# A Mamba block followed by linear attention on one core: the folds of the scanned states put first, TensorE's side work kept to its budget, and ScalarE's passes limited to two in a slot

## The chip, the core and the metric

The kernel runs on one NeuronCore of a Trainium2 chip. TensorE (PE, with its weight loads as PEld), VectorE (DVE), ScalarE (ACT) and GpSimd (POOL) each work off their own queue of instructions in order; SyncE (SP) issues most transfers. The metric is the device time of one execution, in microseconds (us), as the median of several runs. The kernel before takes 7723.51 us (median of three runs, 7722.88 to 7725.43).

## What is computed

The input is x, 4 batches of 512 channels by 4096 positions, in float32. Two layers, each added to its own input, with a norm over groups of 16 channels ahead of each:

```python
# layer 0, for each group of 128 channels ("chunk")
xn = layer_norm(group_norm(x))            # over 512 channels
xi, z = split(xn_chunk @ in_proj)         # 256 + 256 channels
xc = silu(causal_conv4(xi) + conv_b)
dt, B, C = split(xc @ x_proj);  dt = softplus(dt @ dt_proj + dt_b)
h[l] = exp(dt[l] * A) * h[l-1] + (dt[l] * xc[l]) * B[l]     # 256 channels x 16 states
y[l] = sum over states of h[l] * C[l]  +  xc[l] * D
x = x + proj(layer_norm(out_proj(y * silu(z)) + skip * xn_chunk))
# layer 1
q, k, v = group_norm(x) @ w_qkv;  q, k = relu(q), relu(k)
x = x + w_out @ ((v @ (k^T q)) / norm)    # linear attention, 8 heads
```

The recurrence over l is the heart: 4 batches x 4 chunks x 256 channels x 16 states, each a chain over 4096 positions.

## The kernel before

**Slots.** Positions are cut into tiles of 512. A *step* is one (batch, tile, chunk): 128 steps in all. A step has 16 *slots*: two halves `e` of the 256 channels, four groups `q` of four states, two halves `jj`. In each slot (`slot`, L837) VectorE makes two scans of 128 rows x 512 positions (L846), each from a decay `dA` that ScalarE makes in PSUM (`decay`, L820, three ahead, three banks) and an input `bx` that GpSimd makes (`drive`, L828, two slots ahead, three buffers).

**Pairs.** Two slots make a *pair*, with one buffer `h` of four scanned rows of 512; there are two such buffers. The states of a pair are then multiplied by C: positions 0 to 383 by VectorE (`product`, L866) with `c_all`, which TensorE spreads into the one bank of `ps_c` (`c_row`), and positions 384 to 511 by GpSimd (L858). Then TensorE adds them up over the states into the bank `y` with four small matmuls (`fold_states`, `y<-h,fold`). The product and the fold of a pair are issued in the first slot of the next pair, after its first scan, but after its second scan in slot 10. So the scan that opens pair k must wait until the fold of pair k-2, which reads the same `h`, is done; that fold is queued one pair earlier, behind its product. In `fold_states` the order on TensorE is: `c_row` for the next pair; where a half `e` begins (the folds issued in slots 2 and 10) also `diagonal`, four small matmuls that start bank `y` with xc * D; then the four folds. `take_y` (ScalarE, slots 0 and 8) reads the one bank `y` out.

**The work around the scans.** All else is written out by hand in `after` (L1323), which runs at the end of each slot: the projections of the step after next (slots 3 to 9), time steps with two table loads around a softplus (slot 3), out-projection (slot 4), a silu with two table loads (slot 10), and so on. Three queues of generators give further pieces: `ahead` (norms of the next tile), `late` (norm and projection of the finished tile) and `rest` (the attention of the batch before). In every slot each queue may give one piece, if its last `yield` allows it: kind "free" goes always, "wide" only at set slots, and other pieces of `late` and `rest` only while `credit` is positive. `credit` gains 3.5 matmuls a slot less what was spent, at most 2.6. A piece of kind "more" (the second half of a group of four matmuls) also goes without credit, if no other queue has issued more than one matmul in the slot. In the slots after 3 and 10 a "free" piece may go twice. `clear` (L108) keeps ScalarE's norm and statistics passes out of slots 3 and 10 (`AWAY`). The passes are L397 (group norm, in two groups of two), L474 and L515 (squares), L485 (layer norm's scale) and L661 (sums and squares for the next norm). `fetch` (L929) lets a tile for the attention land for two slots before it is used.

After the last slot the attention of the last batch runs alone, nearly all of it on TensorE.

Of the kernel before, what the change touches and what calls it, by code (L numbers as in the profile page):

```python
# [8 lines left out]
F32 = mybir.dt.float32  # L9
# [5 lines left out]
P = 128  # L15
T = 512
# [8 lines left out]
def kernel(  # L25
# [48 lines left out]

    held, now, due = [0], [None], []

    def work_bank(name, behind=1):
        held[0] += behind  # L80
# [26 lines left out]

    def clear():  # L108

        while now[0] is not None and now[0] % SLOTS in AWAY:  # L110
            yield "wait"

    def pause(n):
        return until(later(n, lambda: None))
# [272 lines left out]
    def group_norm(dst, xt, norm):  # L387
        gr, off, _ = norm
        for c in range(NC):
            if c % 2 == 0:  # L390
                yield from clear()
            if now[0] is None and c % 2:
                nc.vector.tensor_scalar(
                    dst[:, c, :], xt[:, c, :], gr[:, c : c + 1], off[:, c : c + 1], ALU.mult, ALU.add
                )
            else:
                nc.scalar.activation(  # L397
                    dst[:, c, :], xt[:, c, :], AF.Identity,
                    bias=off[:, c : c + 1], scale=gr[:, c : c + 1],
                )  # L400
            if c == 1:
                yield "free"
        yield
# [53 lines left out]
    def layer_norm(v, name):  # L457
        while norming:
            yield "wait"
        norming.append(name)  # L460
        yield from room()
        sums = work_bank(f"mu_sums_{name}")
        sums_into(sums, [v[:, c, :] for c in range(NC)], range(NC))
        mu = yield from mean_of(sums, f"mu_{name}", "one ahead")
        yield "wide"
        over(v, mu, ALU.subtract)
        free()
        yield "free"
        sqs = []
        for c in range(NC):  # L470
            if c % 2 == 0:
                yield from clear()
            sqs.append(wk.tile([P, T], F32, tag="sq", name=f"sq_{name}_{c}", bufs=4))
            nc.scalar.activation(sqs[c], v[:, c, :], AF.Square)  # L474
            if c == 1:
                yield "free"
        yield from room()
        sums = work_bank(f"var_sums_{name}")
        sums_into(sums, sqs, range(NC))
        var = yield from mean_of(sums, f"var_{name}", "two ahead")  # L480
        yield from over_deviation(v, var, name)
        for c in range(NC):
            if c % 2 == 0:
                yield from clear()
            nc.scalar.activation(  # L485
                v[:, c, :], v[:, c, :], AF.Identity,
                bias=b_sb[:, c : c + 1], scale=g_sb[:, c : c + 1],
            )
            if c % 2:
                yield "free"  # L490

    def layer_scale(v, name):
# [19 lines left out]

        def part(c):
            sqs[c] = wk.tile([P, T], F32, tag="sq", name=f"sq_{name}_{c}", bufs=4)
            nc.scalar.activation(sqs[c], v[:, c, :], AF.Square, bias=about)  # L515

        yield from clear()
# [127 lines left out]
    def shifted(f, xt, t, nm):  # L645
# [11 lines left out]
        for o in range(NC):  # L657
            yield from clear()
            for v, func in (("sum", AF.Identity), ("square", AF.Square)):
                unused = wk.tile([P, T], F32, tag="res", name=f"{v}_{nm}_{o}", bufs=2)  # L660
                nc.scalar.activation(  # L661
                    unused, xt[:, o, :], func, bias=f["off"][:, o : o + 1],
                    accum_out=f[v][:, o, t : t + 1],
                )
            yield "free"
# [202 lines left out]
    def fold_states(g, last):  # L868

        n, e, q, _ = place(g)  # L870
        if g + 1 < last:
            c_row(g + 1)
        if q == 0:
            ys[n, e] = ps_y.tile([P, T], F32, tag="y", name=f"y_{n}_{e}")
            diagonal(ys[n, e], dg[:, e, :], fs[n]["xz"][:, 0, e, :])
        h = hs.pop(g // JJ)
        for j in range(NJ):
            mm(
                ys[n, e][j * BLK : (j + 1) * BLK, :], fold, h[:, j, :],
                start=False, stop=(q == NQ - 1), abreast=NJ,  # L880
            )


    def take_y(f, n, e):
        nc.scalar.copy(f["xz"][:, 0, e, :], ys.pop((n, e)))  # L885
# [31 lines left out]
    def attention(b, x1s, stats):  # L917
# [12 lines left out]
        def fetch(t, why, spare=1):  # L930

            if t < NT and t not in tiles and not no_tile(spare):
                x1 = load_now(x1s[t], f"x{why}_{b}_{t}")
                tiles[t] = x1, pause(2)

        def fetched(t, why):
            fetch(t, why)
# [365 lines left out]
    with tc.manual_schedule():  # L1303
        credit, seen, mix, held[0], held_x[0] = 0.0, work["mm"], iter(()), 0, 0
        for n, (b, t, c) in enumerate(steps):
# [10 lines left out]
            for s in range(SLOTS):  # L1316
                def after():
                    nonlocal credit, seen
                    now[0] = n * SLOTS + s
                    for what in [w for at, w in due if at <= now[0]]:  # L1320
                        what()
                    due[:] = [d for d in due if d[0] > now[0]]
# [130 lines left out]
```

## Time and profile before

| | |
|---|---|
| median of 3 runs | 7723.51 us |
| the profiled execution | 7720.72 us, of it a span of 7718.9 us |
| mean granted TensorE clock | 0.914 |
| busy: PE / DVE / ACT / POOL | 83% / 90% / 71% / 89% of the span |
| scans run from / to | 91.6 us / 7293.4 us |
| the four batches, from first scan to the next batch's first | 1757.6, 1815.9, 1815.9, 1810.0 us |
| after the last scan | 425.5 us |

A page gives busy times over the whole span; here some 92 us at the start and 425 us at the end belong to other work, so VectorE and GpSimd are fuller in the loop than the page's shares. In the lists of waits, a row gives the waiting engine and line, who ended the wait, the total, the number and the longest. In the timelines the columns are start, length, engine, line, operation, tiles, shapes and count, and in brackets the idle time of the engine just before and who ended it. A matmul of 128x512 float32 stands there as two records.

### The profile page before, as it was taken

How to read it: one execution, taken by the hardware profiler on the slowest of the kernel's cores; microseconds unless marked ns; L12 is line 12 of the kernel's file. 1: busy time of each engine (PE TensorE's matmuls, PEld its weight loads, DVE VectorE, ACT ScalarE, POOL GpSimd, SP SyncE). 2: the span in 40 equal slices, each digit the busy share in tenths (PEclk: the TensorE clock that was granted, in tenths of full speed). 3: DMA queues.
4: the chain of work that ended last, by engine and by line, in shares of the span. 5: the costliest groups of instructions: out<-in, count | busy, mean ns of one | idle time of the engine just before them, and what ended most of it. 6: DMA issues, size and time to landing. Idle time of an engine off the chain costs nothing.

```text
span 7718.9 us, 91874 instructions
## 1 busy us (share of the span) xinstructions
PE 6424.2 (83%) x25496; PEld 2090.3 (27%) x25528; DVE 6951.6 (90%) x5720; ACT 5466.3 (71%) x8384; POOL 6892.8 (89%) x4638
## 2 busy tenths in 40 slices
PE   5677777677789988988788988898788889898799
PEld 1111212111223322322222333332122323232244
DVE  6999999999999999999999999999999999999821
ACT  5677777777777777777777777777777777777521
POOL 5999999999999999999999999999999999999700
PEclk8788888888899999999899999999899999999799
DMA  6666666666666666676666666677666665677502
GB/s 176 168 171 168 158 151 160 163 159 169 174 171 169 164 170 167 181 196 168 175 167 174 178 165 163 164 187 194 161 172 165 161 161 150 168 191 192 141 33 93
DMA packets 829222, 1265.43 MB, mean 164 GB/s; under 512 B 184072, under 2 KB 317720, under 8 KB 816416
## 3 DMA queue, kind: packets, MB, share of 16 engines
q1 hardware_dynamic: 806352, 1225.99, 60.8%
q0 software_dynamic: 16368, 32.51, 2.4%
q8 instruction: 200, 3.28, 0.2%
q14 instruction: 318, 2.61, 0.1%
q10 hardware_dynamic: 5984, 1.06, 0.1%
HBM read 1052.25 MB, written 206.57 MB: 163 GB/s over the span
## 4 chain that ended last, share of the span: by engine, by line
DVE 35%; PE 29%; ACT 11%; DMA 8%; issue 7%; POOL 7%; SPq 2%; DVEq 0%; POOLq 0%; ACTq 0%
DVE h L846 22%; DVE h L866 10%; PE pc L129 6%; PE y L129 5%; PE pq L129 5%; POOL bx L828 5%; ACT dA L820 4%; DMA d_all<-d_rows 3%; PE pr L129 3%; PE po L129 3%; PE pp L129 2%; SPq L795 2%; DVE xn L439 2%; DMA c_sb<-c_rows 2%; DMA b_all<-b_rows 1%
## 5 line engine op out<-in xcount | busy, mean ns | idle before, releaser
L828 POOL TENSOR_TENSOR bx<-d_all,b_all 128x1024 f32<-128x1024 f32 x2048 | 4824.6, 2368 | 147.2 <-DVE h L846 130.3
L846 DVE TENSOR_TENSOR_SCAN h<-dA,st,bx 128x512 f32<-128x512 f32 x3584 | 4352.3, 1267 | 309.7 <-ACT dA L820 101.9
L820 ACT ACTIVATE dA<-d_all,a_t 128x512 f32<-128x512 f32 x4096 | 2756.9, 688 | 1408.1 <-DVE h L846 1351.8
L866 DVE TENSOR_TENSOR h<-h,c_all 128x1536 f32<-128x1536 f32 x1024 | 1770.5, 1729 | 0.1
L858 POOL TENSOR_TENSOR h<-h,c_sb 128x512 f32<-128x512 f32 x1024 | 1299.8, 1269 | 99.7 <-DMA c_sb<-c_rows 15.9
L129 PE MATMUL y<-h,fold 128*32 128x512 f32 x8192 | 1249.3, 685 | 43.9 <-POOL h L858 42.3
L129 PE MATMUL c_all<-parts,sel 128*128 128x384 bf16 x1024 | 366.1, 358 | 939.2 <-DVE h L866 936.8
L129 PE MATMUL pc<-xn,w_cv 128*128 128x512 f32 x2048 | 1037.4, 640 | 129.1 <-DVE xn L439 79.7
L129 PE MATMUL pq<-w_qk,xa 128*128 128x512 f32 x2048 | 953.3, 601 | 5.1 <-ACT xa L397 2.5
L846 DVE TENSOR_TENSOR_SCAN h<-dA,bx 128x512 f32<-128x512 f32 x512 | 590.7, 1205 | 39.0 <-PE y L129 15.7
L129 PEld LDWEIGHTS pc<-xn,w_cv 128*128 128x128 f32 x2048 | 385.0, 199 | 735.3 <-issue 408.1
L129 PEld LDWEIGHTS <-sel 128*128 128x128 bf16 x1216 | 120.4, 99 | 1606.3 <-DVE h L866 1392.2
L129 PEld LDWEIGHTS pq<-w_qk,xa 128*128 128x128 f32 x2048 | 389.8, 193 | 453.7 <-issue 435.6
L129 PE MATMUL pr<-xb,m 128*128 128x512 f32 x1024 | 475.8, 603 | 3.4 <-ACT res L1136 2.6
L129 PE MATMUL pp<-xn,w_pr 128*128 128x512 f32 x1024 | 477.4, 596 | 0.0
L129 PE MATMUL y<-xz,dg 32*32 32x512 f32 x2048 | 346.2, 752 | 0.0
L888 POOL TENSOR_TENSOR xz<-xz 128x512 f32<-128x512 f32 x256 | 325.4, 1271 | 11.2 <-ACT xz L885 11.2
L129 PEld LDWEIGHTS y<-h,fold 128*32 128x32 f32 x8192 | 169.6, 113 | 611.5 <-issue 381.4
L731 POOL TENSOR_TENSOR dt<-dt,xz 128x1024 f32<-128x1024 f32 x127 | 299.9, 2361 | 0.8 <-ACT dt L723 0.6
L129 PE MATMUL pd<-xz,w_xp 128*128 128x512 f32 x512 | 294.7, 704 | 0.0
L129 PE MATMUL pz<-xn,w_z 128*128 128x512 f32 x512 | 271.5, 623 | 6.5 <-ACT kq L959 4.8
L129 PEld LDWEIGHTS pr<-xb,m 128*128 128x128 f32 x1024 | 192.8, 193 | 253.9 <-issue 226.9
(226 smaller groups left out, 5965.4 us busy)
## 6 DMA issues: line engine op xcount, KB each, us to landing
d_all<-d_rows SPq DMA_DIRECT2D x2040, 256.0 KB, 4.3
b_all<-b_rows SPq DMA_DIRECT2D x4096, 64.0 KB, 2.4
d_rows<-dt SPq DMA_DIRECT2D x254, 512.0 KB, 2.8
c_sb<-c_rows SPq DMA_DIRECT2D x4096, 16.0 KB, 3.5
xn<-in_x_dram SPq DMA_DIRECT2D x32, 1024.0 KB, 7.1
x<-xr SPq DMA_DIRECT2D x32, 1024.0 KB, 4.2
xa<-x SPq DMA_DIRECT2D x32, 1024.0 KB, 5.2
xb<-x SPq DMA_DIRECT2D x32, 1024.0 KB, 5.8
```

The lines of the kernel that those rows point to most:

```text
L129: nc.tensor.matmul(out_, lhsT, rhs, **how)
L439: nc.vector.tensor_tensor(v, v, bc(m, NC), op)
L731: nc.gpsimd.tensor_tensor(f["both"][:, 1], f["both"][:, 0], f["xz"][:, 0], ALU.mult)
L795: nc.sync.dma_start(dst[k * BLK : (k + 1) * BLK, :], rows_[q * KS + k, :].partition_broadcast(BLK))
L820: nc.scalar.activation(dAs[k], fs[n]["d_all", e][:, 0, j, :], AF.Exp, scale=a_t[:, e, j, q : q + 1])
L828: nc.gpsimd.tensor_tensor(bxs[g], fs[n]["d_all", e][:, 1, jj * 2 : jj * 2 + 2, :], bc(b_all[g // JJ], 2), ALU.mult)
L846: nc.vector.tensor_tensor_scan(h[:, j, :], dAs.pop(2 * g + i), bxs[g][:, i, :], 0.0 if t == 0 else st[:, c, e, q, j : j + 1], ALU.mult, AL ...
L858: nc.gpsimd.tensor_tensor(h[:, :, CUT:], h[:, :, CUT:], bc(c_sb.pop(g // JJ), NJ), ALU.mult)
L866: nc.vector.tensor_tensor(own, own, bc(c_all.pop(g // JJ), NJ), ALU.mult)
L888: nc.gpsimd.tensor_tensor(f["xz"][:, 1, e, :], f["xz"][:, 1, e, :], f["xz"][:, 0, e, :], ALU.mult)
```

## The change

There are five edits.

1. `fold_states`: the four folds come first, `c_row` for the next pair after them. `diagonal` leaves this function and becomes `begin_y`, called at the end of slots 1 and 9, after all other pieces of the slot.
2. In slots 3 to 8 (`heavy`) a new piece of `late` or `rest` needs a credit above 1 instead of above 0, and a "more" piece needs a credit above 0.
3. `fetch` lets a tile land for three slots instead of two.
4. A counter `passes`, cleared in each slot and raised by each of ScalarE's norm and statistics passes of whatever queue.
5. `clear` also holds a generator back, with kind "free", while `passes` is above 1; it is asked before each group of passes.

```diff
     def clear():
-        while now[0] is not None and now[0] % SLOTS in AWAY:
-            yield "wait"
+        while now[0] is not None and (now[0] % SLOTS in AWAY or passes[0] > 1):
+            yield "wait" if now[0] % SLOTS in AWAY else "free"
...
+                passes[0] += 1
                 nc.scalar.activation(
                     dst[:, c, :], xt[:, c, :], AF.Identity,
...
         n, e, q, _ = place(g)
-        if g + 1 < last:
-            c_row(g + 1)
-        if q == 0:
-            ys[n, e] = ps_y.tile([P, T], F32, tag="y", name=f"y_{n}_{e}")
-            diagonal(ys[n, e], dg[:, e, :], fs[n]["xz"][:, 0, e, :])
         h = hs.pop(g // JJ)
         for j in range(NJ):
             mm(
                 ys[n, e][j * BLK : (j + 1) * BLK, :], fold, h[:, j, :],
                 start=False, stop=(q == NQ - 1), abreast=NJ,
             )
+        if g + 1 < last:
+            c_row(g + 1)
+
+    def begin_y(n, e):
+        ys[n, e] = ps_y.tile([P, T], F32, tag="y", name=f"y_{n}_{e}")
+        diagonal(ys[n, e], dg[:, e, :], fs[n]["xz"][:, 0, e, :])
...
-                tiles[t] = x1, pause(2)
+                tiles[t] = x1, pause(3)
...
                     now[0] = n * SLOTS + s
+                    passes[0] = 0
...
-                    busy = False
+                    busy, heavy = False, int(3 <= s < 9)
...
-                        if queue is ahead or kind == "free" or credit > 0 or kind == "more" and not busy:
+                        if queue is ahead or kind == "free" or credit > (kind != "more") * heavy or kind == "more" and not (busy or heavy):
...
+                    if s % (SLOTS // NH) == 1:
+                        begin_y(n, s // (SLOTS // NH))
                     seen = work["mm"]
```

The line `passes[0] += 1` also stands before each of the passes at L474, L485, L515 and L661 (the last with two passes a group).

More of the change, by code (lines that the diff above doesn't have):

```diff
@@ L73 @@
     ps_w = ctx.enter_context(tc.tile_pool(name="ps_w", bufs=3, space=bass.MemoryType.PSUM))
-    held, now, due = [0], [None], []
+    held, now, due, passes = [0], [None], [], [0]
     def work_bank(name, behind=1):
@@ L473, in layer_norm @@
             sqs.append(wk.tile([P, T], F32, tag="sq", name=f"sq_{name}_{c}", bufs=4))
+            passes[0] += 1
             nc.scalar.activation(sqs[c], v[:, c, :], AF.Square)
@@ L484, in layer_norm @@
                 yield from clear()
+            passes[0] += 1
             nc.scalar.activation(
@@ L514, in part @@
             sqs[c] = wk.tile([P, T], F32, tag="sq", name=f"sq_{name}_{c}", bufs=4)
+            passes[0] += 1
             nc.scalar.activation(sqs[c], v[:, c, :], AF.Square, bias=about)
@@ L659, in shifted @@
             for v, func in (("sum", AF.Identity), ("square", AF.Square)):
+                passes[0] += 1
                 unused = wk.tile([P, T], F32, tag="res", name=f"{v}_{nm}_{o}", bufs=2)
```

## The prediction

> **What bounds the kernel now.** First the page's busy line and its groups, to see which engines are full.
>
> ```profile
> PE 6424.2 (83%) x25496; PEld 2090.3 (27%) x25528; DVE 6951.6 (90%) x5720; ACT 5466.3 (71%) x8384; POOL 6892.8 (89%) x4638
> L828 POOL TENSOR_TENSOR bx<-d_all,b_all 128x1024 f32<-128x1024 f32 x2048 | 4824.6, 2368 | 147.2 <-DVE h L846 130.3
> L846 DVE TENSOR_TENSOR_SCAN h<-dA,st,bx 128x512 f32<-128x512 f32 x3584 | 4352.3, 1267 | 309.7 <-ACT dA L820 101.9
> ```
>
> VectorE and GpSimd are nearly equally full, and the loop of 2048 slots takes 7202 us (91.6 to 7293.4). Of VectorE's idle time some 349 us stand before the scans (309.7 here, 39.0 in the group without `st`). That is all there is to win on VectorE, so the second view is its list of waits:
>
> ```profile
> DVE h L846 <- PE y L129: 114.1, 112, 4.5
> DVE h L846 <- ACT dA L820: 104.6, 110, 3.5
> DVE h L846 <- POOL st L857: 38.7, 43, 2.2
> DVE h L846 <- ACT xn L899: 28.4, 30, 2.7
> DVE h L846 <- POOL bx L828: 26.4, 34, 2.2
> DVE h L846 <- ACT kq L954: 22.5, 8, 3.0
> ```
>
> A scan waits on several semaphores, and the named line is only the last event near its start: no scan needs L899, L954 or slot 11's L857. So I paired the trace's 4096 scans in order of issue with their dA, bx and the fold of the pair two back, and took for each idle stretch what ended last. From the third pair on, VectorE's idle time before scans is 346 us: **fold late 234.5, dA late 87.8, bx late 22.3**. By the slot of the waiting scan the folds cost 80.4 (slot 12), 87.9 (slot 8), 22.8 (slot 10), 18.2 (6), 14.7 (4) and 10.6 (the rest); dA costs 29.5 (5), 10.6 (6), 7.3 (7), 8.1 (10), 7.1 (12), 23.2 (13), 2 elsewhere.
>
> Third, the timeline shows why. Slots 4 to 8 of a step with attention:
>
> ```profile
> 2204.09 1.98 PE L129 MATMUL po<-xz,w_op 128*128 128x512 f32 x4
> 2204.53 1.73 DVE L866 TENSOR_TENSOR h<-h,c_all 128x1536 f32<-128x1536 f32 x1
> ...
> 2205.91 1.88 PE L129 MATMUL pp<-xn,w_pr 128*128 128x512 f32 x4
> ...
> 2211.06 0.33 PE L129 MATMUL c_all<-parts,sel 128*128 128x384 bf16 x1
> ...
> 2211.32 1.06 PE L129 MATMUL y<-h,fold 128*32 128x512 f32 x8
> ...
> 2212.55 1.28 DVE L846 TENSOR_TENSOR_SCAN h<-dA,st,bx 128x512 f32<-128x512 f32 x1 [2.74 <-ACT xn L899]
> ```
>
> The product ends at 2206.26, but TensorE is still at out-projection and side work and begins the fold 5.06 us later; the scan starts 0.17 us after the fold's end. Without stall the scan comes 3.46 us after the product (three scans; 2.37 us for slot 10's fold, which has two). Slot 10's fold:
>
> ```profile
> 3017.71 0.34 PE L129 MATMUL c_all<-parts,sel 128*128 128x384 bf16 x1
> 3017.97 1.06 PE L129 MATMUL y<-xz,dg 32*32 32x512 f32 x8
> 3018.97 1.06 PE L129 MATMUL y<-h,fold 128*32 128x512 f32 x8
> ```
>
> Even begun at once, it ends 2.4 us after its product, against 2.37 us of room. And dA: six passes in one slot hold ScalarE's queue (first column start, second length):
>
> ```profile
> 2966.97 0.71 ACT L661 ACTIVATE sum<-xr,moff 128x512 f32<-128x512 f32 x1
> 2968.38 2.92 ACT L397 ACTIVATE xa<-xa,off_b,gr_b 128x512 f32<-128x512 f32 x4
> 2971.91 1.28 DVE L846 TENSOR_TENSOR_SCAN h<-dA,st,bx 128x512 f32<-128x512 f32 x1 [3.47 <-ACT dA L820]
> ```
>
> **The change part by part.** No arithmetic is added or removed; the instructions of each kind are as many, but for about 1010 more semaphore waits each on PE and VectorE (the fold now waits for VectorE itself, the product for `c_row`). VectorE's recurring order keeps its slots, so this is about TensorE's and ScalarE's places.
>
> *Folds first, diagonals a slot earlier.* The fold of slot 10 starts 0.26 + 1.00 us sooner after its product, and so does slot 2's. Subtracting 1.4 us (the two rows' lengths) from each of the 78 stalls of slot 12 leaves 10.4 of 80.4 us, and behind them 6.3 of dA show up: 16. Slot 4: 14.7 to 0. Elsewhere a fold gains 0.34 us. `c_row` is now 1.06 us later, but its product comes a scan after the next fold's deadline: nothing. The diagonal goes to the end of slots 1 and 9, where TensorE had on average 1.0 and 2.4 us of work; it waits for `take_y` of the slot before, behind which only that slot's `c_row` and fold are queued: nothing, or if ScalarE is late the wait it had before.
>
> *No overdraft.* Counting each slot's matmuls at the rows' lengths (0.94 us for 128x512 float32, 1.06 for four small ones) in the two orders, for batches 1 and 2: slots 2 to 4 fall from 12.8 to 10.9 us (the slots take 11.8), slots 5 to 9 go from 15.4 to 16.8 (17.4). Runs of three slots with over 12 us of matmuls fall from 202 to 124. Slot 6's fold, behind slots 2 to 5, comes 0.34 us sooner by its order and up to 1.9 by the load: stall at slot 8 87.9 becomes 20 (subtracting 1.4 from each of its 66 stalls; 11 with 1.9, 66 with 0.34). Slot 8's fold has 0.7 us more before it in slots 6 and 7 and less backlog: 22.8 becomes 17. Slots 6, 14, 0: 7 of 29. Folds in all: 234.5 to 60, a gain of 175; with the order's 0.34 us alone for slots 6, 8, 10 and 14 it is 120.
>
> *Two passes a slot.* Slots with four or more passes fall from 103 to none (one has three). The excess of six passes over two is 4 x 0.7 to 0.8 = 3 us, as large as the stalls of 1.3 to 3.5 us at slot 13: 23 becomes 5; slot 6's, up to 2.8 us behind four passes, go from 10.6 to 3. Slot 5's dA waits for slot 3's table loads, begun late because a `pq` queued behind slot 2's diagonal was late: 1.06 us sooner takes 29.5 to about 5, of 27 stalls up to 2 us. The other 24.5 stay: dA 88 to 37, gain 51. Held passes shift the next tile's norm by one slot, and attention ends at slot 1011 instead of 992 (batch 0's), with 76 slots to spare; batch 2's at 2024 of 2048. The tail has the same 130 ScalarE instructions: 0.
>
> *Longer landing.* The chain of waits has three `xb` landings of 8.1 to 9.8 us, over two slots (7.1): 0 to 5 us. I take 0, since TensorE's waits name no DMA.
>
> *More semaphore waits.* Those before the scans take 21 ns each: 1010 on VectorE cost 0 to 21 us. I take 0, as they pass while the previous scan runs (back-to-back starts overlap by 83 ns with and without one).
>
> **Where the stall goes.** Gross the sum is 175 + 51 = 226 us. What is late next is GpSimd. Its idle time by batch is 45.6, 90.8, 90.4, 90.3 us; 81 ns lie between each `st` copy and the product behind it, 20.7 us a batch, and can't be won. So 25, 70, 70 and 70 us: 235 us is the most that the loop can gain, with GpSimd never waiting. It shares three buffers with VectorE and meets long rows of its own (L731 in slot 4, the gates in 1 and 9), so I leave it some 1% idle: 8 us in batch 0, 20 in the others. Net gain 17 + 3 x 50 = 167 us; bx stalls grow by the difference, 59, to some 80. The profiled execution, 7720.7, becomes 7554; the median before is 2.8 us higher: **7556**.
>
> **A rule against it.** The Trainium skill, "TensorE: Matmul & The Clock Gate", Part 1, says that the array falls to half clock after an idle window of about 3.4 us. The trace agrees in size: a fold takes 1.06 us and at times 1.94, and the granted clock is 0.84 between 1000 and 2000 us but 0.95 in the next 1000. By the rule the budget, which thins TensorE's bursts, might cool it: with every fold at 1.94 the stalls of slots 8 and 10 would grow by 0.88 x 79 = 70 us, and the gain be 97. By the row I expect no more cold folds: the same work in a shorter loop, and the diagonal fills the idle slot 1.
>
> **Rivals.** (1) *Half relief* (0.22): TensorE keeps late, since attention's side work is held to 3.5 matmuls or 3.3 us a slot, 95% of a 3.45 us slot, and cold stretches come on top. Fold relief 120 less the cold 70, dA 40: 90 net, 7634. For it: 83% busy, 66 stalls at slot 8. Against: load of slots 2 to 4 falls below their time. (2) *Slower* (0.09): what leaves slots 3 to 5 lands in slots 6 to 9 (14.1 us against 12.5; they take 14.5 now, 13.5 without stalls). If the backlog that enters slot 6 does not shrink, the folds of slots 8 and 10 begin 2 us later in some 82 attention steps. They end on average 1.08 and 0.73 us before their scan, so each step loses 0.92 + 1.27 = 2.19 us: 180 us, less the relief of slots 12 and 13 (64 + 18) and batch 0's 17: +81, 7804. It decides from 1.5 us later on. Against: the total before slot 10's fold is 0.7 us smaller than now. (3) *GpSimd binds wholly* (0.06): 7490 to 7505, TensorE no longer late at all. (4) That passes are not held is excluded by the new order.
>
> **Chances.** The forecast (7515 to 7600) 0.59, half relief (7600 to 7690) 0.22, GpSimd alone 0.06, slower 0.09, within 0.2% (15 us, about what a measurement tells from no change) 0.04. So faster 0.87. The range 7495 to 7660 leaves out the slower and unchanged cases and some of the half relief and of rival 3.
>
> **What would show it.** Idle before L846 from 349 to 150-180 us, with `PE y` (and the false names L899, L954, L857) far down and POOL bx the largest; L828's idle before it halved; slot 12's stall nearly gone right with the fold directly behind the product; no stall at slot 13. Wrong: `PE y` waits moved to slots 10 and 12 (rival 2), cold folds more frequent, or the granted clock lower.

## The result and the profile after

| | before | after |
|---|---|---|
| median of 6 runs each, same chip | 7724.47 us (7720.18 to 7730.03) | 7662.35 us (7652.55 to 7665.79) |
| ratio, 95% interval | | 0.9919 (0.9906 to 0.9931) |
| profiled execution | 7720.7 us | 7665.6 us |
| scans run from / to | 91.6 / 7293.4 us | 95.0 / 7238.4 us |
| VectorE idle before scans: fold / dA / bx late | 234.5 / 87.8 / 22.3 us | 140.3 / 77.7 / 68.0 us |
| time at half TensorE clock | 1325 us | 1547 us |

The change gains 62 us, not the 167 that were forecast; the time lies just outside the range, near the "half relief" rival. The page of the changed kernel, its busy line and the groups that answer to those of before (total and mean length, then the idle time ahead of them and who ended most of it):

```profile
PE 6445.6 (84%) x25507; PEld 2129.9 (28%) x25528; DVE 6950.2 (91%) x5720; ACT 5455.4 (71%) x8384; POOL 6890.5 (90%) x4638
...
L833 POOL TENSOR_TENSOR bx<-d_all,b_all 128x1024 f32<-128x1024 f32 x2048 | 4825.1, 2369 | 105.5 <-DVE h L851 85.9
L851 DVE TENSOR_TENSOR_SCAN h<-dA,st,bx 128x512 f32<-128x512 f32 x3584 | 4351.8, 1267 | 252.7 <-PE y L129 99.0
```

The scans have as much work as before (4351.8 us) and less idle time ahead of them: 252.7 us for 309.7. GpSimd still waits 105.5 us ahead of `bx` (147.2 before), so it is not full either. VectorE's list of waits:

```profile
DVE h L851 <- PE y L129: 109.0, 104, 3.1
DVE h L851 <- ACT dA L825: 82.8, 131, 3.1
DVE h L851 <- POOL bx L833: 72.8, 84, 4.2
```

The false names (L899, L954, L857) are nearly gone, but the folds (`PE y`) are still first. Paired as for the prediction (each scan with its own dA, bx and fold), the idle time by the slot of the waiting scan, in us:

| waiting scan | late | before | forecast | after |
|---|---|---|---|---|
| slot 12, first | fold | 80.4 | 10, and 6 of dA behind it | 26.2 |
| slot 8 | fold | 87.9 | 20 | 52.0 |
| slot 6 | fold | 18.2 | 4 | 35.7 |
| slots 4, 10 | fold | 37.5 | 17 | 22.9 |
| slot 13 | dA | 23.2 | 5 | 4.7 |
| slot 5 | dA | 29.5 | 5 | 25.7 |
| slot 12, second | dA | 7.1 | 7 (unchanged) | 29.3 |
| all | bx | 22.3 | 80 | 68.0 |
| all | all | 346 | 177 | 287 |

The same step whose slot 8 was shown in the prediction looks like this now (TensorE's rows, with VectorE's product and the scan that waits). The product ahead of slot 6's fold ends at 2202.59:

```profile
2199.32 1.98 PE L129 MATMUL po<-xz,w_op 128*128 128x512 f32 x4
2200.86 1.73 DVE L871 TENSOR_TENSOR h<-h,c_all 128x1536 f32<-128x1536 f32 x1
2201.14 1.88 PE L129 MATMUL pp<-xn,w_pr 128*128 128x512 f32 x4
2202.86 1.88 PE L129 MATMUL pc<-xn,w_cv 128*128 128x512 f32 x4
2204.57 1.88 PE L129 MATMUL pp<-xn,w_pr 128*128 128x512 f32 x4
2206.38 1.06 PE L129 MATMUL y<-h,fold 128*32 128x512 f32 x8
...
2207.62 1.28 DVE L851 TENSOR_TENSOR_SCAN h<-dA,st,bx 128x512 f32<-128x512 f32 x1 [1.49 <-PE y L129]
```

The fold starts 3.79 us after its product (5.06 before), the scan waits 1.49 us (2.74). Two pieces of the projection (`pp`) still stand in front of it: in this step the budget lets them through.

### The profile page after: what moved, and what is told of

Read it like the earlier page. It is cut to its first block, busy times and chain, and to the rows that moved or that the text cites. A ratio compares the mean times of both kernels' runs of the same rounds, so it can differ in the third digit from the quotient of the medians.

```text
span 7663.9 us, 93895 instructions
## 1 busy us (share of the span) xinstructions
PE 6445.6 (84%) x25507; PEld 2129.9 (28%) x25528; DVE 6950.2 (91%) x5720; ACT 5455.4 (71%) x8384; POOL 6890.5 (90%) x4638
## 3 DMA queue, kind: packets, MB, share of 16 engines
q10 hardware_dynamic: 5984, 1.06, 0.1%
## 4 chain that ended last, share of the span: by engine, by line
PE 28%; DVE 23%; DMA 13%; ACT 12%; issue 9%; POOL 9%; SPq 5%; POOLq 0%; DVEq 0%; ACTq 0%
DVE h L851 14%; DVE h L871 7%; PE pc L129 7%; POOL bx L833 6%; ACT dA L825 5%; DMA d_all<-d_rows 5%; DMA c_sb<-c_rows 4%; PE pq L129 4%; PE y L129 4%; SPq L800 4%; PE pp L129 3%; PE pr L129 3%; PE po L129 2%; DMA b_all<-b_rows 2%; DVE xn L440 2%
## 5 line engine op out<-in xcount | busy, mean ns | idle before, releaser
L833 POOL TENSOR_TENSOR bx<-d_all,b_all 128x1024 f32<-128x1024 f32 x2048 | 4825.1, 2369 | 105.5 <-DVE h L851 85.9
L851 DVE TENSOR_TENSOR_SCAN h<-dA,st,bx 128x512 f32<-128x512 f32 x3584 | 4351.8, 1267 | 252.7 <-PE y L129 99.0
L129 PE MATMUL y<-h,fold 128*32 128x512 f32 x8192 | 1267.8, 685 | 850.7 <-DVE h L871 472.0
L129 PE MATMUL pc<-xn,w_cv 128*128 128x512 f32 x2048 | 1109.1, 673 | 151.6 <-DVE xn L440 100.8
L129 PEld LDWEIGHTS y<-h,fold 128*32 128x32 f32 x8192 | 186.2, 113 | 1702.2 <-POOL h L863 880.5
L129 PEld LDWEIGHTS pc<-xn,w_cv 128*128 128x128 f32 x2048 | 412.5, 210 | 712.1 <-issue 430.7
L129 PE MATMUL y<-xz,dg 32*32 32x512 f32 x2048 | 317.1, 691 | 32.5 <-ACT xz L891 32.0
L736 POOL TENSOR_TENSOR dt<-dt,xz 128x1024 f32<-128x1024 f32 x127 | 300.1, 2363 | 0.6 <-ACT dt L728 0.6
```

The source lines that it names most:

```text
L129: nc.tensor.matmul(out_, lhsT, rhs, **how)
L736: nc.gpsimd.tensor_tensor(f["both"][:, 1], f["both"][:, 0], f["xz"][:, 0], ALU.mult)
L833: nc.gpsimd.tensor_tensor(bxs[g], fs[n]["d_all", e][:, 1, jj * 2 : jj * 2 + 2, :], bc(b_all[g // JJ], 2), ALU.mult)
L851: nc.vector.tensor_tensor_scan(h[:, j, :], dAs.pop(2 * g + i), bxs[g][:, i, :], 0.0 if t == 0 else st[:, c, e, q, j : j + 1], ALU.mult, AL ...
```

## The experiments

The first runs (e1 to e4, then e6 to e9) set three theories against each other. *Fixed blocks*: ScalarE's table blocks and TensorE's wait in slot 3 stay where they are, so that what a fold gains comes back as the next scan's wait. *Cold clock*: the change thins TensorE's bursts, and TensorE runs slower. *GpSimd binds*: what is won comes back as bx lateness. None of them fitted all of these runs, and from e10 on two others were tested: *the order theory*, by which the diagonal at the end of slots 1 and 9 still stands ahead of the next fold in TensorE's queue and holds it, and the *credit* that the moved diagonals no longer use. The prediction had taken the diagonal's new place as free. Times are medians, ratios are to the kernel before on the same chip. As the runs were made on several chips, differences between kernels are to be read from the ratios. The stalls and the half-clock times come from one profiled execution of each kernel.

| kernel | time, us | ratio (95%) | fold / dA / bx late, us | half clock, us |
|---|---|---|---|---|
| e1_order | 7732.0 | 1.0012 (1.0006 to 1.0018) | 210 / 74 / 73 | 1530 |
| e2_budget | 7697.7 | 0.9965 (0.9954 to 0.9977) | 192 / 89 / 35 | 1332 |
| e3_passes | 7721.9 | 0.9997 (0.9989 to 1.0005) | 204 / 102 / 39 | 1308 |
| e4_no_passes | 7676.6 | 0.9936 (0.9924 to 0.9948) | 135 / 98 / 68 | 1482 |
| e10_order_behind | 7666.9 | 0.9926 (0.9912 to 0.9939) | 113 / 127 / 50 | 1301 |
| after | 7662.4 | 0.9919 (0.9906 to 0.9931) | 140 / 78 / 68 | 1547 |
| e11_diag_ahead | 7664.3 | 0.9920 (0.9907 to 0.9934) | 131 / 75 / 90 | 1499 |
| e12_diag_end | 7664.0 | 0.9921 (0.9907 to 0.9934) | 119 / 101 / 72 | 1513 |
| e14_charged | 7662.8 | 0.9918 (0.9905 to 0.9932) | 133 / 75 / 86 | 1492 |
| e15_behind_uncharged | 7639.4 | 0.9892 (0.9879 to 0.9906) | 90 / 119 / 63 | 1353 |
| e7_diag_behind | 7628.9 | 0.9873 (0.9860 to 0.9887) | 73 / 117 / 66 | 1277 |
| e6_warm | 7654.0 | 0.9905 (0.9892 to 0.9919) | 126 / 86 / 68 | 1240 |
| e13_fill2 | 7658.0 | 0.9915 (0.9901 to 0.9928) | 131 / 89 / 67 | 1243 |
| e8_no_loads3 | 7644.4 | 0.9895 (0.9882 to 0.9909) | 119 / 49 / 107 | 1479 |
| e9_u_late | 7661.5 | 0.9914 (0.9900 to 0.9927) | 127 / 77 / 83 | 1595 |
| e16_hold3 | 7684.6 | 0.9948 (0.9936 to 0.9961) | 99 / 121 / 96 | 1356 |
| e17_behind_hold3 | 7678.7 | 0.9946 (0.9932 to 0.9959) | 61 / 135 / 92 | 1219 |
| e19_hold25 | 7671.2 | 0.9922 (0.9908 to 0.9935) | 141 / 80 / 76 | 1493 |
| e18_behind_hold25 | 7624.9 | 0.9869 (0.9855 to 0.9882) | 77 / 110 / 72 | 1284 |

**The parts alone.** e1 is the kernel before with edit 1 alone, e2 with edit 2 alone, e3 with edits 4 and 5 alone; e4 is the changed kernel with edits 4 and 5 undone (edit 3, the landing, was not run by itself):

```diff
 # e4, against the kernel after
-        while now[0] is not None and (now[0] % SLOTS in AWAY or passes[0] > 1):
-            yield "wait" if now[0] % SLOTS in AWAY else "free"
+        while now[0] is not None and now[0] % SLOTS in AWAY:
+            yield "wait"
```

> Only the first edit: folds ahead of c_row, diagonals at the end of slots 1 and 9. Theory of fixed blocks (ScalarE's table blocks of slots 3 and 10 and TensorE's wait for a free bank in slot 3 are not moved by the change, so what a fold gains there comes back as the next scan's own wait): slot 12's fold stall falls from 80 to about 25 us, but 20 us or more of it comes back as a dA stall of slot 12's second scan; slots 6 and 8 keep over 90 us of fold stall; about 7690 us. Theory of the cold clock (moving work out of slots 2 and 10 thins TensorE's bursts): the half-clock time in this run alone rises from 1325 to 1500 us or more, slot 4 of batch 0 goes cold, and the batch 0 gain is under 10 us. Theory that GpSimd binds: bx stalls rise from 22 to over 60 us already here.

> Only the second edit, the budget of slots 3 to 8. Fixed blocks: a gain of at most 20 us (7705 to 7720), slot 8's fold stall 88 to about 65, slot 6's not smaller. Cold clock: this is the edit that cools TensorE, half-clock time rises to 1500 us or more here and hardly in the run with the order alone. GpSimd binds: no more than 10 us of bx stall beyond 22, since little is won.

> Only the two passes a slot (the counter and the condition in clear). Fixed blocks: slot 13's dA stall falls from 23 to about 5 us, slot 6's from 11 to near 0, slot 5's 29 stays, as it stands behind slot 3's table loads; gain 15 to 25 us (7700 to 7709). Cold clock and GpSimd: no change in half-clock time or bx stalls.

> The whole change without the two passes a slot. Fixed blocks: 10 to 20 us slower than the whole change (7672 to 7682); slot 13's dA stall is back at 20 us or more, slot 12's second scan keeps 20 us or more of dA stall. Cold clock: half-clock time as in the whole change, about 1550 us. GpSimd binds: no slower than the whole change by more than 5 us, as GpSimd is the limit in both.

The order alone gains nothing (0.12% slower). Slot 12's stall does fall, 80 to 33 us, but slot 8's rises from 88 to 102, slot 6's from 18 to 31, and bx lateness from 22 to 73. The budget alone takes slot 8 from 88 to 38 us and gains 0.35%. The passes alone take slot 13's dA from 23 to 8 us and gain nothing that can be measured, because slot 5's dA grows from 29.5 to 45 and bx by 17, as much as the folds lose (30). Together the edits give 0.81%, more than the sum of the three (0.26%). The folds' reliefs nearly add up: 24, 42 and 30 us alone, 94 together. What does not add up is bx: each edit alone makes it later, by 51, 13 and 17 us, and all together by 46. Why, no run shows.

Of the three theories, fixed blocks had the stalls of slots 12 and 13 about right and all three gains wrong (e1 was to gain some 35 us, e2 at most 20, e3 15 to 25). The cold clock was looked for in the order and in the budget; it came with the order (1530 us at half clock in e1) and not with the budget (1332 in e2, 1325 before). GpSimd's bx did rise above 60 us in e1.

e4 shows what the pass limit does within the whole: without it slot 13's dA is 15.7 us (4.7 with it), slot 6's 10.1 (under 2), slot 12's second scan's 38.1 (29.3), but slot 5's only 13.9 (25.7). The limit itself makes dA late at slot 5, as it did in e3.

**The place of the diagonal.** In e7 the first fold of a half begins the bank, and the diagonal is added directly behind the fold and `c_row`, in slots 2 and 10; it counts against the credit again, as before:

```diff
+        if q == 0:
+            ys[n, e] = ps_y.tile([P, T], F32, tag="y", name=f"y_{n}_{e}")
         h = hs.pop(g // JJ)
         for j in range(NJ):
             mm(
                 ys[n, e][j * BLK : (j + 1) * BLK, :], fold, h[:, j, :],
-                start=False, stop=(q == NQ - 1), abreast=NJ,
+                start=(q == 0), stop=(q == NQ - 1), abreast=NJ,
             )
         if g + 1 < last:
             c_row(g + 1)
+        if q == 0:
+            diagonal(ys[n, e], dg[:, e, :], fs[n]["xz"][:, 0, e, :], False)
...
-                    if s % (SLOTS // NH) == 1:
-                        begin_y(n, s // (SLOTS // NH))
```

> The whole change, but bank y is begun by the first fold, and the diagonal is added behind that fold and c_row, in slots 2 and 10 (the same sum in another order). Cold clock: TensorE's burst in slot 2 is whole again, half-clock time falls back from 1547 to about 1350 us, slot 4 of batch 0 is warm, and the kernel is 15 to 25 us faster than the whole change (about 7640). GpSimd binds locally or fixed blocks: within 6 us of the whole change (7662), with bx stalls at slot 8 as before.

e10 is the same order put into the kernel before, without edits 2 to 5:

> The kernel before with the folds first, c_row behind them, and the diagonal added behind c_row in slots 2 and 10, so that bank y is begun by the fold: each slot's matmuls and side pieces are those of before, only their order within slots 0, 2, 4 and so on differs. Place in the queue (the diagonal at the end of slots 1 and 9 still stands in front of the next fold and delays it): slot 12's fold stall falls from 80 to under 10 us, and the kernel gains 30 to 45 us (7685 to 7695), where the order with moved diagonals gained nothing. Cold clock: half-clock time stays near 1325 us, same gain. GpSimd binds locally: bx stalls at slot 8 rise to 40 us, gain under 12 us.

e7 is the fastest kernel but for e18, which is no different within the intervals: 7628.9 us. Its scans end at 7194.1 us (7238.4 after). Slot 12's fold stall is 1.9 us in e7 and 1.1 in e10. e10 and e1 differ in the diagonal's place and its counting alone, and lie 66 us apart: the order theory holds (e10 gains 57 us, where 30 to 45 were expected). The gain of e7 and its half-clock time (1277 us) are also about what the cold clock had forecast for it; the runs with filler below tell the two apart. VectorE's list of waits in e7:

```profile
DVE h L851 <- ACT dA L825: 121.9, 152, 2.4
DVE h L851 <- POOL bx L833: 67.9, 87, 4.5
DVE h L851 <- PE y L129: 59.9, 71, 2.6
```

Here the folds have become the last of the three and ScalarE's dA the first.

Four kernels split the difference between e7 and the kernel after. e14 is the kernel after with the moved diagonals counted against the credit, which makes its side pieces the same in each slot as e7's; e12 has the diagonal at the end of slots 2 and 10, uncounted; e15 has it directly behind `c_row`, uncounted; e11 has it ahead of the fold in slots 2 and 10, as the kernel before has, with `c_row` last:

```diff
 # e14, against the kernel after
+                    seen = work["mm"]
                     if s % (SLOTS // NH) == 1:
                         begin_y(n, s // (SLOTS // NH))
-                    seen = work["mm"]
 # e12, against e7, at the end of the slot in place of fold_states
+                    if s % (SLOTS // NH) == 2:
+                        e_ = s // (SLOTS // NH)
+                        diagonal(ys[n, e_], dg[:, e_, :], f["xz"][:, 0, e_, :], False)
                     seen = work["mm"]
 # e15, against e7
+            was = work["mm"]
             diagonal(ys[n, e], dg[:, e, :], fs[n]["xz"][:, 0, e, :], False)
+            work["mm"] = was
 # e11, against the kernel after, in fold_states; the call in slots 1 and 9 goes
+        if q == 0:
+            begin_y(n, e)
         h = hs.pop(g // JJ)
```

> The whole change with the moved diagonals charged to the credit of their slots, as they were before (one line moved): attention then ends at slot 1050 instead of 1011 of batch 1. Credit: 10 to 20 us faster than the whole change, with slot 4's and slot 6's folds sooner. Place in the queue or cold clock: within 6 us of 7662, half-clock time not below 1500 us.

> The whole change with the same side pieces in the same slots, but the diagonal at the end of slots 2 and 10, behind the fold, instead of at the end of slots 1 and 9. Place in the queue or cold clock: 20 us or more faster than the whole change (7640 or less), slot 12's fold stall under 6 us, half-clock time under 1400 us; slot 5's dA stall stays near 26 us, since pt and pq now stand ahead of the diagonal. Credit (the moved diagonals are charged to no slot's budget, so more side work gets in): no more than 8 us from 7662.

> The kernel after, with the diagonal directly behind the fold and c_row in slots 2 and 10, but not counted against the credit. Theory (the place in TensorE's queue is what counts: ahead of the next fold nothing may stand, and the diagonal fills the gap behind the fold while slot 3's first matmul waits for its bank): as e7, 7620 to 7645 us, fold stalls of slot 12 under 5 us and of slot 6 near 21. Rival (it is the credit: e7's diagonals are counted and so thin the side work behind them): as e12, 7655 to 7670, with slot 6's fold stall at 40 to 56 us and slot 12's second scan near 45.

> The kernel after, with the diagonal ahead of the fold in slots 2 and 10 as in the kernel before, c_row behind the fold. Theory (it is the diagonal's place against the fold that counts): the fold of slot 10 starts 1.0 us later than in e7, so slot 12's fold stall is 20 to 40 us, and the time 7640 to 7665. Rival (only the end of slots 1 and 9 is bad, and ahead of the fold in its own slot is as good as behind): slot 12 under 10 us, and within 10 us of e7, 7620 to 7640.

- e14 (0.9918) equals the kernel after: the credit alone is worth nothing. Against e7, with identical pieces in each slot, the place is worth 35 us.
- e11 (0.9920) equals it too, with the same stall at slot 12 (27.5 us; 26.8 in e14, 26.2 after). So the move to the end of slots 1 and 9 did nothing that can be measured. What took slot 12 from 80 to some 27 us is then, by elimination, `c_row` going last (the budget alone, e2, leaves 72; a kernel with `c_row` last and no other edit was not run). Before, `c_row` needed the product's end, as there is one bank for `c_all`, and held the diagonal and the fold that were queued behind it. This row of the groups shows that wait on the kernel before:

```profile
L129 PE MATMUL c_all<-parts,sel 128*128 128x384 bf16 x1024 | 366.1, 358 | 939.2 <-DVE h L866 936.8 <-ACT parts L776 0.6
```

  and on the kernel after, where the fold waits for the product itself and `c_row` for nothing:

```profile
L129 PE MATMUL y<-h,fold 128*32 128x512 f32 x8192 | 1267.8, 685 | 850.7 <-DVE h L871 472.0 <-POOL h L863 340.4 <-POOL xz L894 32.7
...
L129 PE MATMUL c_all<-parts,sel 128*128 128x384 bf16 x1024 | 374.4, 366 | 0.6 <-ACT parts L781 0.6
```

- e12 (0.9921) frees slot 12's first scan (2.0 us) and gains nothing: slot 12's second scan then waits 46.7 us for dA (29.3 after), and slot 6 waits 55.8 us for its fold (35.7). At the end of slot 2 the diagonal stands behind that slot's side pieces and ahead of slot 4's fold.
- e15 (0.9892) moves it directly behind `c_row` and gains 22 us on e12, and 21 on the kernel after: slot 6's stall is 34.4 us. Counting it against the credit as well (e7) gives some 15 us more, which is near the intervals' limit (each about 10 us either way).

The timeline shows what the place does. Slots 2 to 4 of one attention step, kernel after:

```profile
2128.62 1.06 PE L129 MATMUL y<-xz,dg 32*32 32x512 f32 x8
2131.30 1.06 PE L129 MATMUL y<-h,fold 128*32 128x512 f32 x8 [1.62 <-POOL xz L894]
...
2132.56 1.13 PE L129 MATMUL pt<-dt,w_dt 32*128 32x512 f32 x4
2136.93 3.78 PE L129 MATMUL pc<-xn,w_cv 128*128 128x512 f32 x4 [3.24 <-DVE xn L440]
2140.64 1.87 PE L129 MATMUL mu_sums_b<-xn,ones 128*32 128x512 f32 x8
2142.33 1.03 PE L129 MATMUL y<-h,fold 128*32 128x512 f32 x8
```

and the same slots of the same step in e7:

```profile
2122.53 1.07 PE L129 MATMUL y<-h,fold 128*32 128x512 f32 x8
2123.53 0.34 PE L129 MATMUL c_all<-parts,sel 128*128 128x384 bf16 x1
2123.80 1.06 PE L129 MATMUL y<-xz,dg 32*32 32x512 f32 x8
2124.79 1.13 PE L129 MATMUL pt<-dt,w_dt 32*128 32x512 f32 x4
2125.84 1.98 PE L129 MATMUL pc<-xn,w_cv 128*128 128x512 f32 x4
2127.76 1.06 PE L129 MATMUL mu_sums_b<-xn,ones 128*32 128x512 f32 x8
2128.64 1.04 PE L129 MATMUL y<-h,fold 128*32 128x512 f32 x8
```

In this step slot 3's first matmul (`pc`) starts only when VectorE's norm product (L440) has ended, so the work ahead of it, done sooner, leaves TensorE idle: 3.24 us in the kernel after, behind which `pc` takes 3.78 us in place of 1.98. The two stretches are not alike in all else: in e7 side work holds slot 2's fold until 2.6 us behind its product, in the kernel after it starts at once. The granted clock in the two kernels from `pc` to the fold, in the stretches' rows (after, then e7; first the stretch and its length, then each engine's busy time with its count, and behind these the granted clock):

```profile
2136.90:2143.30 6.40, 6.37 (x21) 1.70 (x21) 6.36 (x5) 4.49 (x7) 6.40 (x4) 0.58 0.46 167
```

```profile
2122.50:2128.60 6.10, 6.10 (x34) 1.56 (x34) 6.10 (x5) 5.70 (x8) 6.02 (x5) 1.00 0.57 149
```

0.58 against 1.00. Slot 4's fold starts 2.6 us behind its product in the kernel after and 0.2 us in e7. Over the attention steps (some 80) TensorE's idle time between the folds of slots 2 and 4 is 1.33 us before, 1.67 after and 0.98 in e7, of which the wait for L439 (L440) is 0.88, 1.02 and 0.61.

That wait is found in chunks 1 and 2 alone, while 10 of the 17 us by which slot 6's stall grew lie in chunks 0 and 3 (from 11.5 to 21.7 us). There `pc` waits for ScalarE's softplus (`dt`, L723 before, L728 after), the middle of slot 3's block with its two table loads. TensorE's list of waits, before:

```profile
PE pc L129 <- DVE xn L439: 79.7, 53, 2.3
PE pc L129 <- ACT dt L723: 11.4, 11, 1.7
```

and after:

```profile
PE pc L129 <- DVE xn L440: 100.8, 55, 3.2
PE pc L129 <- ACT dt L728: 39.0, 22, 2.5
```

The second wait grew more (by 28 us) than the first (by 21).

**The clock.** If the slower clock were the cause, filler would win the time back. e6 runs `c_row` four more times in slots 0, 2, 12 and 14 of batch 0 and of the first steps after it; e13 three more times in slots 2 and 10 of all steps. Both only repeat a matmul into the same bank:

```diff
         mm(got, sel[:, q, :], fs[n]["parts"], start=True, stop=True)
+        if q == 1:
+            for _ in range(3):
+                nc.tensor.matmul(got, sel[:, q, :], fs[n]["parts"], start=True, stop=True)
```

> The whole change, and in batch 0 (its steps and the first four after it) the c_row matmul issued five times instead of once in slots 0, 2, 12 and 14, with the same result each time: filler that keeps TensorE busy where it idles. Cold clock: batch 0's half-clock time falls from 734 us to under 400, its fold stall from 20 to under 5 us, and batch 0 from 1751 to about 1738 us. GpSimd binds locally (long rows of slots 1 and 4 make bx late at slot 8): fold stalls fall, but bx stalls of batch 0 rise by as much and batch 0 stays within 4 us of 1751. Fixed blocks: as GpSimd, with no effect after batch 0 either.

> The whole change with c_row issued four times instead of once in slots 2 and 10 (same result), 1.0 us of filler as long as the diagonal that used to stand there; nothing else moves. Cold clock: half-clock time falls from 1547 to 1350 us or less, the folds of slots 4 and 6 start 0.3 us or more sooner after their products, and the kernel gains 12 us or more. Place in the queue: no gain, within 6 us of 7662, or slower, since the filler delays pt and the side piece.

Half-clock time falls from 1547 to 1240 and 1243 us, below the 1325 of before, and the times by 11 and 3 us, both inside the intervals. In batch 0, where e6 has its filler, half-clock time falls from 734 to 464 us and the batch from 1751.1 to 1748.1 us. e13 has filler as long as the diagonal and in the same place as e7's, is warmer than e7, and does not gain e7's 35 us. So the clock is a by-product: its price is not told apart from nothing here, with intervals of about 10 us either way.

**dA and bx.** e8 leaves out slot 3's two table loads, with Exp in place of Softplus (another function of the time step); e9 moves L736, GpSimd's product of 2.36 us in slot 4, to slot 8:

```diff
 # e8
-                        nc.scalar.preload_act_table_set("softplus")
                         time_steps(nxt, names[n + 1])
-                        nc.scalar.preload_act_table_set("natural_log_exp_and_others")
 # e9
                         to_rows(nxt, 0, names[n + 1])
-                        to_rows(nxt, 1, names[n + 1])
+                    if s == 8 and nxt is not None:
+                        to_rows(nxt, 1, names[n + 1])
```

> The whole change with Exp in place of Softplus in the loop and without slot 3's two table loads (it leaves those loads out and computes another function of the time step). ScalarE's block in slot 3 shrinks from 3.8 to 1.3 us. Fixed blocks: slot 5's dA stall of 26 us goes, slot 6's fold stall of 36 us falls below 25, and the kernel gains 25 us or more (about 7635). GpSimd binds locally: slot 5's stall goes too, but half or more of it comes back as bx stall at slots 6 to 8; gain under 12 us.

> The whole change with GpSimd's long product dt * xc (2.36 us a step) issued in slot 8 instead of slot 4, its two stores and loads behind it. GpSimd binds locally: slot 8's bx stall falls from 44 to under 15 us and the kernel gains 20 us or more (7640 or less). Fixed blocks or cold clock: slot 8's bx stall falls, but its fold stall of 52 us takes its place or bx stalls come up at slots 10 to 12; within 10 us of 7662.

Slot 3's block in one step of the kernel after, and the scan of slot 5 that waits for it:

```profile
2924.16 1.28 ACT L1343 ACT_TABLE_LOAD   x1
2925.46 1.26 ACT L728 ACTIVATE dt<-pt,dtb 128x512 f32<-128x512 f32 x2
2926.74 1.28 ACT L1345 ACT_TABLE_LOAD   x1
2928.04 1.30 ACT L825 ACTIVATE dA<-d_all,a_t 128x512 f32<-128x512 f32 x2
...
2928.76 1.28 DVE L851 TENSOR_TENSOR_SCAN h<-dA,st,bx 128x512 f32<-128x512 f32 x1 [1.02 <-ACT dA L825]
```

e8 takes slot 5's dA stall from 25.7 us to 0: without the table loads nothing of it is left. When the block begins still counts. Its first softplus comes on average 4.85 us behind slot 3's first scan before, 4.73 after and 5.06 in e7, where the diagonal stands ahead of `pt` and the stall is 55 us. Slot 6's fold stall falls in e8 too, from 36 to 20 us (in chunks 0 and 3 from 21.7 to 7.2), as expected if `pc` waits for this block. The time falls by only 18 us: dA falls by 29 us and the folds by 21, but bx rises by 39.

```profile
DVE h L851 <- POOL bx L833: 106.4, 113, 4.0
DVE h L851 <- PE y L129: 89.8, 89, 6.0
DVE h L851 <- ACT dA L825: 55.4, 96, 1.7
```

With one engine relieved GpSimd's bx is the first row. e9 clears bx at slot 8 (44 to 13 us), and 48 us more of it appear at slot 12 (7 to 55): moving GpSimd's work moves the wait.

**Slot 3's piece and chunk 2's.** e16 (from after) and e17 (from e7) give no new piece of `late` or `rest` in slot 3, e19 (from after) and e18 (from e7) none in slot 5 of chunk 2's steps:

```diff
 # e16, e17; in e18 and e19 the condition is (c, s) == (2, 5)
                         kind = queue[0][1] if queue else None
+                        if s == 3 and queue is not ahead and kind != "free":
+                            continue
```

> The kernel after, with no new piece of the late and rest queues in slot 3. Theory (slot 3's side piece stands ahead of slot 4's fold on TensorE and waits there for a bank or for its data): fold stall of slot 6 from 36 to under 20 us, and the time 7635 to 7655, since some of it comes back at bx and dA. Rival (the piece only moves to slots 4 and 5, ahead of slot 6's fold): slot 6 lower but slot 8 higher by as much, 7655 to 7675.

> e7 (diagonal behind c_row, counted) with no new piece of late and rest in slot 3. Theory (two separate reliefs): slot 6's fold stall from e7's 21 to some 10 us, and 7610 to 7630 us. Rival (what is relieved here is taken back by dA of slot 5 and by bx of slot 8, which are next): 7625 to 7645, no faster than e7.

> The kernel after and no new piece of the late and rest queues at the end of slot 5 in steps of chunk 2. Theory: slot 8's fold stall from 52 to some 10 us, and the time 7630 to 7655. Rival (moved to the next fold, or taken back by bx at slot 8 and by slot 12's dA): 7655 to 7675.

> e7 (diagonal directly behind c_row) and no new piece of the late and rest queues at the end of slot 5 in steps of chunk 2. Theory (the projection piece in front of slot 6's fold is what stalls slot 8 there): slot 8's fold stall from 33 to under 10 us; as GpSimd's bx is late at the same scan in part of these steps, the time falls by 5 to 20 us, 7610 to 7625. Rival (the piece is only in front of the next fold then): slot 10's stall grows by as much, 7625 to 7640.

e16 and e17 lose 22 and 56 us against their own bases, and neither reading held. Slot 6's stall is 36.4 us in e16 (35.7 after) and 31.1 in e17 (21.1 in e7), but by chunk it has moved: in chunks 0, 1 and 3 together it falls from 23.7 to 0.4 us (16.2 to 0.4 in e17), as the first reading had it, and in chunk 2 it rises from 12.1 to 35.9 (4.9 to 30.7). There hardly any side piece stands between the folds of slots 2 and 4 any more, and `pc` waits 2.3 us a step (1.8 in e17) for ScalarE's L728 with slot 4's fold behind it. The held pieces come later: dA stalls 41.6 and 31.2 us at slot 15 (8 and 9 before the edit), bx 27 and 26 at slot 12 (from 7), and the stretch after the last scan is some 9 us longer. e18 and e19 follow another trail. Sorted by chunk, slot 8's fold stall is

| | chunk 0 | chunk 1 | chunk 2 | chunk 3 |
|---|---|---|---|---|
| before | 15.5 | 43.6 | 26.2 | 2.6 |
| after | 0 | 7.0 | 44.0 | 1.0 |
| e19_hold25 | 1.1 | 7.6 | 7.0 | 1.0 |

The counts of TensorE's records between slot 4's fold and slot 6's go with it: side work falls from 9.1 records a step to 0.4 in chunk 0, but only from 6.1 to 5.8 in chunk 2, where the projection runs (`pp` 4.3 before, 4.6 after; 1.9 in e19). Held back one slot, it stalls the next fold: slot 10's stall in chunk 2 goes from 0.6 to 37.8 us, and the time does not change. The rival is right; e18 shows the same (27.7 to 1.4 at slot 8, 0.6 to 26.3 at slot 10).

## Why the prediction was wrong

The sign was right, and the size was not: the loop became 58 us shorter and not 167, as the stalls kept 287 us and not 177. The 110 us are 80 of folds and 41 of dA, less 12 by which bx was forecast too high.

- **The diagonal's new place, put at "nothing": failed.** The prediction let the fold start 1.26 us sooner, 1.00 of it by the diagonal's move (and subtracted 1.4 from each stall; 1.26 would have left 12.9 us and not 10.4). By e11 the diagonal's move gave none of it. Of the 26 us that are left 21 are in chunk 2, where slot 10's fold starts on average 1.9 us behind its product, 0.9 in e7: the difference is about the diagonal's length. I had counted TensorE's work in slots 1 and 9 (1.0 and 2.4 us) and not what was still queued from slot 8. With the diagonal behind the fold slot 12 keeps 1 to 2 us, and the kernel is 21 us faster, 35 with the diagonal counted against the credit.
- **"Slots 2 to 4 fall from 12.8 to 10.9 us" so slot 6's fold comes up to 1.9 us sooner: failed.** A sum of lengths takes TensorE to be working all the time. Slot 3's `pc` waits for VectorE's L440 or ScalarE's L728, so a part of the time freed in slot 2 became idle time (0.34 us a step). Slot 6's own stall doubled (18 to 36 us; 4 was forecast as its share). Slot 8's fell to 52 us and not 20: taking 1.4 us from each of its 66 stalls treated all chunks alike, while chunk 2's grew from 26 to 44 us.
- **Slot 5's dA, "29.5 to about 5": failed.** Slot 3's block was to begin 1.06 us sooner and began 0.12 us sooner. And the pass limit, put at nothing here, makes slot 5's dA late: by 15 us alone (e3), by 12 in the whole (13.9 in e4, 25.7 after). By what way is not shown.
- **What is late next at the same scan: half seen.** I looked for the next cause of the scan that was relieved and not for the next scan. Slot 12's second scan had hidden behind the first; its dA stall went from 7.1 to 29.3 us. The timeline points at slot 10's block with two table loads (no run left it out):

```profile
2837.14 1.28 ACT L1220 ACT_TABLE_LOAD   x1
2838.43 1.48 ACT L1220 ACTIVATE xz<-xz 128x1536 f32<-128x1536 f32 x1
2839.82 0.58 ACT L1221 ACTIVATE xz<-pz 128x512 f32<-128x512 f32 x1
2840.42 1.28 ACT L1365 ACT_TABLE_LOAD   x1
2841.71 0.72 ACT L519 ACTIVATE sq_b<-xn,about 128x512 f32<-128x512 f32 x1
2842.34 1.28 ACT L825 ACTIVATE dA<-d_all,a_t 128x512 f32<-128x512 f32 x2
...
2843.05 2.46 DVE L851 TENSOR_TENSOR_SCAN h<-dA,st,bx 128x512 f32<-128x512 f32 x2 [1.40 <-ACT dA L825]
```

  The block runs from 2837.14 to 2841.70, one pass of the norm follows, and only then the dA that the scan needs.
- **Passes: right where they were looked for.** Slot 13 went from 23.2 to 4.7 us (5 forecast) and slot 6's dA from 10.6 to under 2 (3 forecast). The whole edit gives some 13 us in the combination (e4 against after, at the intervals' limit) and nothing alone.
- **bx and the cap by GpSimd: right in kind.** bx grew to 68 us (80 forecast), and e8 and e9 show it as what comes next.
- **The clock rule.** From the rows I expected no more cold folds. By the Trainium skill's "TensorE: Matmul & The Clock Gate", Part 1, which has the array at half clock after an idle window of about 3.4 us, I feared that the budget might cool it. It did cool, with 1547 us at half clock for 1325, slot 4 of batch 0 alone 105 for 14, but the budget was not the reason (e2: 1332). With the folds ahead of `c_row` the half-clock time is 1479 to 1595 us wherever the diagonal is not directly behind `c_row` (but for the two kernels with filler and e16), and 1219 to 1353 where it is. Folds of over 1.6 us went only from 176 to 196, and e6 and e13 show no price near the 70 us.
- **The rival "half relief"** has the time and half of the reason: TensorE did keep late, but the clock was not what cost. Its 90 us net were 120 of folds and 40 of dA less 70 for the cold array. Measured are 94 of folds and 10 of dA, less 46 by which bx grew.

Left open: why counting the diagonal against the credit gives some 15 us when it stands behind the fold and nothing when it stands ahead (the difference is hardly larger than the intervals); what edit 3 does by itself; why the pass limit makes slot 5's dA late; and whether slot 10's table block is all that holds slot 12's second scan.

## What to carry to other kernels

On an engine that works its queue in order, a small step is free only where nothing that others wait for stands behind it: put the awaited work first, and the filler directly behind it, into a gap that the next instruction's own wait leaves anyway. Before you sum loads, look for the instruction in that stretch that is pinned by another engine; what you free ahead of it can turn into idle time. And sort stalls by slot and by phase of the loop before you subtract a mean relief: here one chunk had 44 of the 52 us that were left, and moving its piece only moved the stall to the next fold.

## What the runs showed of the hardware

- In an idle stretch of 3.24 us TensorE fell to half clock (2.34 us in the same step and slot before the change): four matmul records that take 1.98 us warm took 3.78 us (3.63 before). Both stretches are shorter than the idle window of about 3.4 us that the prediction cites; a shorter gap (1.62 us, and 2.19 before the change) had come some 5 us earlier.
- Repeating one small bfloat16 matmul three times (0.38 us each) in two of sixteen slots took 304 us off the half-clock time and did not change the kernel's time measurably (7658.0 for 7662.4 us).
- The 1010 added waits on VectorE cost nothing that shows: it stands idle 0.1 us in all ahead of its 1024 products, which now wait for `c_row`, in both kernels.
